# Alternating row and column stages in an inverse Haar and convolution round, with filter rows written in longer runs

## The chip, the cores and the metric

The kernel runs on one core of a Trainium2 chip. The metric is the device time of one execution in microseconds (us), the median of several. Five engines run side by side, each working through its own instructions in order: TensorE (PE in the profile; its weight loads are PEld), VectorE (DVE), ScalarE (ACT), GpSimd (POOL) and SyncE (SP). SyncE here only issues DMAs, and it issues nearly all of them. When the instruction at the head of an engine's queue waits for something, everything behind it on that engine waits too.

## The reference

The input x has 4 images of 64 channels of 256 x 256 float32 values. Four layers follow one another:

```python
x = conv(x, L0)      # y = filter * x  + bias * x
x = haar(x, L1)
x = conv(x, L2)
x = conv(x, L3)
```

In a `conv` layer each channel is convolved (causally, cut to 256 x 256) with an outer product of a column filter and a row filter of 256 values each. The filters come from a small network, three layers with a sine and a last product with `Xwo` or `Ywo`, times a decay:

```python
h = sin(freq * (z @ w1 + b1)); h = sin(freq * (h @ w2 + b2)); h = sin(freq * (h @ w3 + b3))
filter = (h @ wo) * exp(-t * abs(deltas))
```

The `haar` layer takes the two-dimensional Haar transform f1 of every channel; for each of two sets i it forms f4 = conv_w[i] mixed over channels of f1 * v[i], shrinks it to sign(f4) * max(|f4| - tau[i], 0), and adds both sets up. The inverse Haar transform of the sum, plus the layer's input, is the output. The Haar transform mixes rows and columns separately, so one direction can be a product with a matrix on TensorE and the other a chain of additions.

## The kernel before

**Units of work.** A round is two channels of two images, a tile of 128 partitions x 8 x 256 values (1 MB). There are 64 rounds (2 groups of images x 32 pairs of channels). A convolution of a round is two stages on TensorE, rows and columns. Each stage is a product with a Toeplitz matrix that is read from DRAM as overlapping slices of the filter (`load_toeplitz`, L146, tile `toep`, four buffers). Each stage is four pieces of 32 matmuls (`toeplitz`, L284); two pieces fill one PSUM group of two banks. After the second, the group is emptied: a row stage by ScalarE copies (L435, L830), a column stage by VectorE, which adds bias times the old value (`residual`, L455, L849). A Haar product is two pieces of eight matmuls (`haar`, L297).

**Phases.** Phase A runs rows and columns of layer 0, the forward additions on GpSimd (L336, L338), the forward product, and a store of the coefficients (`coef`). Phase B mixes channels and shrinks, step by step, for one group of images; it reads `coef` and writes `mixed`. Phase C runs the inverse additions on GpSimd (`inverse_free`, L377; `ci` is the result), the inverse product (P, `c0ps`), layer 2 (`c1r`, `c1c`) and layer 3 (`c2r`, `c2c`), and stores `out`. B for group 0 is interleaved with the second half of A, B for group 1 with the first 29 rounds of C; the rest of C runs alone. For group 1 most of the second set is stored unshrunk by B (`unshrunk`, L669) and is shrunk in the part of C that is alone (`shrink`, L754): a multiply (L772, VectorE), Sign and Abs (L774, L776, ScalarE), a subtraction and a threshold (L778, L781, VectorE), twice per round; GpSimd adds it to `g` (L797).

**Order.** Each phase is a list of small functions, pieces, and the order is written by hand: `beside` (L917) spreads one list evenly between the pieces of another. Nothing reorders instructions afterwards. Each piece first calls `flush` (L390), which emits the emptying of PSUM groups that earlier pieces left with `later`.

**An inverse round before.** In `piece` (L859) of phase C the order is: four row pieces of layer 2 of round t (R1), half of P of round t+1, four row pieces of layer 3 of round t-1 (R2), the other half of P, four column pieces of layer 2 of round t (C1), four column pieces of layer 3 of round t-1 (C2). The loads and stores stand at fixed pieces: `g` of round t+3 at the fifth, both Toeplitz tiles and the unshrunk tile at the sixth, `out` of round t-2 at the eighth. The shrinkage is at the first six pieces and again at the next six; scaling of `g` (`scales`, L350, seven ScalarE operations) is in the last seven pieces.

**PSUM.** Beside B, phase C's groups come from a ring of two; alone, from a ring of three (L955). A group can be written again once its earlier content has been emptied.

**Filters.** Each filter row is written to DRAM `REPEATS` = 20 times, so that a Toeplitz tile can be read as one strided pattern. `spread` (L245) writes one of three items for one of two halves at a time, in runs of 320 values (1280 bytes). The first two rounds' filters have their own path (`repeated`, L214). `last` (L222) is the final product of the filter network.

Of the kernel before, what the change touches and what calls it, by code (L numbers as in the profile page):

```python
# [70 lines left out]
ROUNDS = C // CI  # L71
STEPS = C
# [5 lines left out]
SHRINK = 6  # L78
# [17 lines left out]
def conv_haar_kernel(  # L96
    ctx: ExitStack, tc: tile.TileContext, x, zT, w1, wbd, cols, decay, wo_first, decay_first, bias, forward, inverse, wrow, pack, v, v_rows, out
# [73 lines left out]
    wbd_sb = [constant("wbd0", wbd[:, 0], [P, 3, P])]  # L171
    wo_first_sb = constant("wo_first", wo_first, [P, FIRST, COPIES])
    decay_first_sb = constant("decay_first", decay_first, [COPIES, FIRST, N])
    decay_sb = constant("decay", decay, [P, N])

    def network(ls):
# [45 lines left out]
        def last():  # L222
            ps = mps.tile([P, n, N], F32, tag="ps", name=f"mlp_out{ls[0]}")
            for e, l in enumerate(ls):
                nc.tensor.matmul(ps[:, e, :], wbd_sb[l][:, 2, :], st["h"][:, e, :], start=True, stop=True)
            padded = part("padded", PERIOD)
            nc.vector.memset(padded, 0.0)
            for e, l in enumerate(ls):
                nc.vector.tensor_tensor(padded[:, e, :N], ps[:, e, :], decay_sb, ALU.mult)
                filters[l] = padded[:, e, :]  # L230
# [7 lines left out]
        return pieces + [last]  # L238
# [6 lines left out]
    def spread(l, begin, end, parts):  # L245

        def put(r, k, channel, copies):
            src = filters[l][channel + CI * begin : channel + CI * (end - 1) + 1 : CI].unsqueeze(1)
            times = copies.stop - copies.start
            nc.sync.dma_start(filt[l][begin:end, r, copies, k], src.to_broadcast([end - begin, times, PERIOD]))  # L250

        n = REPEATS // parts
        pieces = []
        for c in range(parts):
            for r in range(2):
                for k in range(ITEMS):
                    channel = k if k < CI else C + r
                    pieces.append(lambda r=r, k=k, at=channel, c=c: put(r, k, at, slice(c * n, (c + 1) * n)))
        return pieces
# [13 lines left out]

    rest = spread(0, 8, 24, 2) + spread(0, 24, ROUNDS, 1)
    rest.append(lambda: wbd_sb.extend(constant(f"wbd{l}", wbd[:, l], [P, 3, P]) for l in (1, 2)))
    rest += network([1, 2])
    rest += spread(1, 0, ROUNDS, 5) + spread(2, 0, ROUNDS, 5)
# [133 lines left out]
    def phase_a():  # L411
# [63 lines left out]
        def piece(t, j):  # L475
            flush()
            if j == 0:
                if t == 0:
                    filters(0)
                    filters(1)  # L480
                    load(0)
                    load(1)
                    for put in spread(0, FIRST, 8, 1):
                        put()
                filters(t + 2)
# [237 lines left out]
    def phase_c():  # L723
# [30 lines left out]
        def shrink(t, k):  # L754
# [11 lines left out]
            if k == 0:  # L766
                s["shrunk"] = late["sb"].tile([P, 2 * M, N], F32, tag="shrunk", name=f"shrunk_{t}", bufs=2)
            for h in range(2):
                j = k - h * SHRINK
                if j == 0:  # L770
                    s["x"] = late["ps"].tile([P, NB, W], F32, tag="x", name=f"x_{t}_{h}")
                    nc.vector.tensor_tensor(s["x"], split("raw", h), rows(0, h), ALU.mult)  # L772
                elif j == 1:
                    nc.scalar.activation(split("shrunk", h), s["x"], AF.Sign)  # L774
                elif j == 2:
                    nc.scalar.activation(s["x"], s["x"], AF.Abs)  # L776
                elif j == 4:
                    nc.vector.tensor_tensor(s["x"], s["x"], rows(1, h), ALU.subtract)  # L778
                elif j == 5:
                    to = split("shrunk", h)  # L780
                    nc.vector.scalar_tensor_tensor(to, s["x"], 0.0, to, ALU.max, ALU.mult)  # L781

        def scaled(t, count):
            if 1 < t < total:
                run(st[t]["scales"], count)
# [72 lines left out]

        def piece(t, j):  # L859
# [5 lines left out]
            if j == 6 and t > 1:  # L865
                store(t - 2)
            if j == BLOCKS:
                filters(t + 1, 1)
                filters(t, 2)
            at = order.index(j)  # L870
            if t >= alone - AHEAD:
                if t == alone - AHEAD and at in (0, 2):
                    (load_raw(alone), load_rows()) if at == 0 else scale_rows()
                if j == BLOCKS:
                    load_raw(t + AHEAD + 1)
                shrink(t + AHEAD, at - 4 * (t == alone - AHEAD))
            if j == 2 * BLOCKS:

                load(t + 3)
            if j < BLOCKS:  # L880
                if t < total:
                    rows(t, 1, j)
            elif j < 2 * BLOCKS:
                if t > 0:
                    rows(t - 1, 2, j - BLOCKS)
            elif j < 2 * BLOCKS + 2:
                product(t + 1, j - 2 * BLOCKS)
            elif j < 3 * BLOCKS + 2:
                if t < total:
                    columns(t, 1, j - 2 * BLOCKS - 2)  # L890
            elif t > 0:
                columns(t - 1, 2, j - 3 * BLOCKS - 2)
            if at > 10 and t < total - 3 and "scales" in st[t + 3]:
                scaled(t + 3, 1 if t > 0 else 2)
# [181 lines left out]
```

## Time and profile before

| | |
|---|---|
| Median of 3 runs | 2650.2 us (2639.0 to 2656.2) |
| Profiled execution, own time | 2654.4 us |
| Its span, first to last instruction | 2652.6 us |
| TensorE matmuls busy | 2357.1 us (89%) |
| GpSimd busy | 2020.8 us (76%) |
| VectorE busy | 1785.2 us (67%) |
| ScalarE busy | 1325.2 us (50%) |
| Mean granted TensorE clock | 0.968 |
| DMA traffic | 684.6 MB, mean 258 GB/s |

In the trace the phases lie at about these places: start until 48 us (first round that runs without a break), A beside the writing of filters until 440, A beside B until 1087, the passage to C until 1224, C beside B until 1909, a passage until 1956, and C alone until the end. The phases have different limits, so a share over the whole span says little; windows of the trace, one for each phase, say more. In a line of groups, the first number is the start or busy time, the second the length, and "idle before" tells how long the engine stood still and what ended it. "issue" means that the profile shows nothing that the engine waited for.

### The profile page before, as it was taken

How to read it: one execution, taken by the hardware profiler on the slowest of the kernel's cores; microseconds unless marked ns; L12 is line 12 of the kernel's file. 1: busy time of each engine (PE TensorE's matmuls, PEld its weight loads, DVE VectorE, ACT ScalarE, POOL GpSimd, SP SyncE). 2: the span in 40 equal slices, each digit the busy share in tenths (PEclk: the TensorE clock that was granted, in tenths of full speed). 3: DMA queues.
4: the chain of work that ended last, by engine and by line, in shares of the span. 5: the costliest groups of instructions: out<-in, count | busy, mean ns of one | idle time of the engine just before them, and what ended most of it. 6: DMA issues, size and time to landing. Idle time of an engine off the chain costs nothing.

```text
span 2652.6 us, 117788 instructions
## 1 busy us (share of the span) xinstructions
PE 2357.1 (89%) x53276; PEld 1901.4 (72%) x53276; DVE 1785.2 (67%) x2040; ACT 1325.2 (50%) x2187; POOL 2020.8 (76%) x2426
## 2 busy tenths in 40 slices
PE   6999999678877778879999999999999999999999
PEld 5777777445554445657787777777888888888888
DVE  2564445799999999656565666665567767766663
ACT  1111112566666666236665566666555555555552
POOL 2788777889989889758666666666788898888881
PEclk9999999889999999889999999999999999999999
DMA  5767777699999889557888788988865566655552
GB/s 184 248 207 275 254 268 266 260 331 325 345 328 334 330 307 332 186 202 275 316 307 311 278 300 295 324 294 316 271 222 190 193 205 207 205 187 193 189 167 99
DMA packets 176006, 684.64 MB, mean 258 GB/s; under 512 B 22487, under 2 KB 35192, under 8 KB 151057
## 3 DMA queue, kind: packets, MB, share of 16 engines
q1 hardware_dynamic: 175505, 677.11, 72.5%
q8 instruction: 418, 6.85, 1.0%
q14 instruction: 83, 0.68, 0.1%
HBM read 427.40 MB, written 249.63 MB: 255 GB/s over the span
## 4 chain that ended last, share of the span: by engine, by line
PE 55%; DVE 15%; POOL 14%; issue 8%; ACT 5%; DMA 3%; SPq 1%; DVEq 0%; ACTq 0%; POOLq 0%
PE c1c L288 10%; PE c2c L288 10%; PE c2r L288 9%; PE c1r L288 8%; POOL fw L336 5%; PE f L596 4%; PE a2ps L288 4%; PE a1ps L288 4%; POOL f L338 4%; PE c0ps L300 3%; DVE a L632 3%; DVE x L455 2%; DVE x L615 2%; DVE m L637 2%; PE a3ps L300 2%
## 5 line engine op out<-in xcount | busy, mean ns | idle before, releaser
L377 POOL TENSOR_TENSOR i<-i,g 128x16 f32<-128x16 f32 x744 | 422.4, 588 | 27.8 <-ACT g L354 0.6
L596 PE MATMUL f<-ft,mix 64*64 64x512 f32 x2048 | 319.3, 641 | 104.7 <-DVE x L615 82.6
L288 PEld LDWEIGHTS a1ps<-toep,x 64*64 64x64 f32 x8192 | 306.1, 139 | 119.7 <-DVE f L468 42.1
L288 PEld LDWEIGHTS c1c<-toep,ch 64*64 64x64 f32 x8192 | 312.8, 134 | 86.5 <-ACT ch L830 35.2
L288 PEld LDWEIGHTS c2r<-toep,cy 64*64 64x64 f32 x8192 | 312.2, 134 | 77.0 <-issue 36.2
L288 PE MATMUL c1c<-toep,ch 64*64 64x192 f32 (+3 forms) x8192 | 337.8, 301 | 26.0 <-issue 13.4
L288 PE MATMUL a1ps<-toep,x 64*64 64x64 f32 (+3 forms) x8192 | 339.2, 308 | 24.1 <-DVE f L468 10.6
L288 PEld LDWEIGHTS a2ps<-toep,ay 64*64 64x64 f32 x8192 | 288.7, 135 | 92.4 <-issue 51.4
L288 PE MATMUL c2r<-toep,cy 64*64 64x192 f32 (+3 forms) x8192 | 330.4, 300 | 26.0 <-issue 22.7
L288 PE MATMUL a2ps<-toep,ay 64*64 64x192 f32 (+3 forms) x8192 | 325.7, 301 | 30.7 <-issue 22.1
L655 POOL TENSOR_TENSOR gt<-m,ft 128x512 f32<-128x512 f32 x128 | 163.4, 1277 | 235.8 <-DVE m L637 235.4
L455 DVE SCALAR_TENSOR_TENSOR x<-x,bias_sb,a2ps 128x512 f32<-128x512 f32 x256 | 179.6, 742 | 223.2 <-POOL f L338 114.9
L288 PE MATMUL c1r<-toep,z 64*64 64x192 f32 (+3 forms) x8192 | 316.5, 298 | 10.5 <-ACT g L354 8.0
L288 PEld LDWEIGHTS c1r<-toep,z 64*64 64x64 f32 x8192 | 297.3, 134 | 38.3 <-issue 15.6
L288 PE MATMUL c2c<-toep,ch 64*64 64x256 f32 (+3 forms) x8192 | 316.9, 297 | 7.9 <-issue 7.5
L377 POOL TENSOR_TENSOR ci<-i,g 128x1024 f32<-128x1024 f32 x124 | 319.8, 2600 | 4.5
L435 ACT COPY ay<-a1ps 128x512 f32<-128x512 f32 x256 | 137.1, 588 | 372.3 <-PE a1ps L288 371.9
L621 ACT ACTIVATE m<-x 128x1024 f32<-128x1024 f32 x194 | 206.1, 1062 | 229.6 <-DVE x L615 170.5
L288 PEld LDWEIGHTS c2c<-toep,ch 64*64 64x64 f32 x8192 | 297.6, 134 | 32.0 <-issue 18.3
L632 DVE TENSOR_TENSOR a<-a,v 128x1024 f32<-128x1024 f32 x192 | 235.5, 1226 | 54.6 <-ACT a L627 54.6
L849 DVE SCALAR_TENSOR_TENSOR cy<-z,bias_sb,c1c 128x512 f32<-128x512 f32 x256 | 177.5, 741 | 136.9 <-PE c1c L288 136.8
L627 ACT ACTIVATE a<-x 128x1024 f32<-128x1024 f32 x194 | 199.9, 1030 | 122.6 <-DVE m L637 122.6
(80 smaller groups left out, 3782.5 us busy)
## 6 DMA issues: line engine op xcount, KB each, us to landing
toep<-filt SPq DMA_DIRECT2D x384, 224.0 KB, 6.1
coef<-f SPq DMA_DIRECT2D x128, 512.0 KB, 6.7
ft<-coef SPq DMA_DIRECT2D x128, 512.0 KB, 7.9
v<-in_v SPq DMA_DIRECT2D x64, 1024.0 KB, 7.2
mixed<-gt SPq DMA_DIRECT2D x128, 512.0 KB, 6.9
g<-mixed SPq DMA_DIRECT2D x128, 512.0 KB, 7.6
x<-in_x SPq DMA_DIRECT2D x63, 1024.0 KB, 6.7
out<-o SPq DMA_DIRECT2D x63, 1024.0 KB, 8.8
```

Source lines behind the costliest of these rows:

```text
L288: nc.tensor.matmul(ps[r][half(c), j % 2, k * ROW :], data[half(r), c, k, bass.ts(j, ROW)], t(r, c)[:, : N - k * ROW], start=k == 0, stop=k ...
L300: nc.tensor.matmul(ps[r][half(c)].rearrange("p h k -> p (h k)"), matrix[half(r)], pairs(r, c).rearrange("p h k -> p (h k)"), start=True, s ...
L336: nc.gpsimd.tensor_tensor(diffs, even, odd, ALU.subtract)
L377: engine.tensor_tensor(to, s, d, op)
L435: later(lambda y=y, ps=ps: nc.scalar.copy(y, ps))
L455: nc.vector.scalar_tensor_tensor(to, old, bias_sb[:, c : c + 1], ps, ALU.mult, ALU.add)
L596: nc.tensor.matmul(un[u]["f4"][half(q), b, :], mixers[0][half(r), bass.ts(i, C)], st[s]["f"][half(r), b], start=True, stop=True, tile_posi ...
L621: nc.scalar.activation(un[u]["m"], un[u]["x"], AF.Sign)
L627: nc.scalar.activation(un[u]["a"], un[u]["x"], AF.Abs)
L632: nc.vector.tensor_tensor(un[u]["a"], un[u]["a"], both(u, "tau"), ALU.subtract)
L655: nc.gpsimd.tensor_tensor(g[:, 0], m[:, 0], st[s]["f"][:, 0], ALU.add)
L849: nc.vector.scalar_tensor_tensor(to, of, bias_sb[:, at : at + 1], ps, ALU.mult, ALU.add)
```

## The change

1. The order in an inverse round becomes R1 (four pieces), first half of P, C2 of round t-2 (four), R2 of round t-1 (four), second half of P, C1 of round t (four). Layer 3's columns thus run one round later than before, and there is one more round of pieces at the end.
2. The shrinkage's ten operations stand at pieces 1, 2, 3, 5, 6 and 10, 11, 12, 14, 15. The scaling of `g` is at pieces 8 (three operations), 9 (two), 15 and 16 (one each).
3. The DMAs of a round are issued at other pieces: `g` at 1, layer 2's Toeplitz tile at 2, the unshrunk tile at 5, `out` at 10, layer 3's Toeplitz tile at 13.
4. `spread` writes all three items of both halves in one DMA, in runs of 960 values (3840 bytes). To have these side by side in one partition, `last` makes three products per layer with 64 output rows in place of one with 128, in pieces of their own, from a separate constant `wo`.

```diff
-SHRINK = 6
+SHRINK = (1, 2, 3, 5, 6, 10, 11, 12, 14, 15)
...
-        def last():
-            ps = mps.tile([P, n, N], F32, tag="ps", name=f"mlp_out{ls[0]}")
-            for e, l in enumerate(ls):
-                nc.tensor.matmul(ps[:, e, :], wbd_sb[l][:, 2, :], st["h"][:, e, :], start=True, stop=True)
-            padded = part("padded", PERIOD)
-            nc.vector.memset(padded, 0.0)
-            for e, l in enumerate(ls):
-                nc.vector.tensor_tensor(padded[:, e, :N], ps[:, e, :], decay_sb, ALU.mult)
-                filters[l] = padded[:, e, :]
+        def last(e, k):
+
+            l = ls[e]
+            if k == 0:
+                filters[l] = mp.tile([HALVES, ITEMS, PERIOD], F32, tag=f"padded{l}", name=f"padded{l}")
+                nc.vector.memset(filters[l], 0.0)
+            ps = mps.tile([HALVES, N], F32, tag="ps", name=f"mlp_out{l}_{k}")
+            nc.tensor.matmul(ps, wo_sb[:, l, k], st["h"][:, e, :], start=True, stop=True)
+            nc.vector.tensor_tensor(filters[l][:, k, :N], ps, decay_sb[:, k], ALU.mult)
...
-        def put(r, k, channel, copies):
-            src = filters[l][channel + CI * begin : channel + CI * (end - 1) + 1 : CI].unsqueeze(1)
-            times = copies.stop - copies.start
-            nc.sync.dma_start(filt[l][begin:end, r, copies, k], src.to_broadcast([end - begin, times, PERIOD]))
+        def put(copies):
+            at = slice(2 * begin, 2 * end)
+            src = filters[l][at].rearrange("p k e -> p (k e)").unsqueeze(1)
+            to = filt[l].rearrange("t h c k e -> (t h) c (k e)")[at, copies]
+            nc.sync.dma_start(to, src.to_broadcast([2 * (end - begin), copies.stop - copies.start, SPAN]))
...
-    rest = spread(0, 8, 24, 2) + spread(0, 24, ROUNDS, 1)
+    rest = [p for q in (8, 16, 24) for p in spread(0, q, q + 8, 2)]
...
-    rest += spread(1, 0, ROUNDS, 5) + spread(2, 0, ROUNDS, 5)
+    rest += spread(1, 0, ROUNDS, 10) + spread(2, 0, ROUNDS, 10)
...
-                    for put in spread(0, FIRST, 8, 1):
+                    for put in spread(0, FIRST, 8, 2):
...
+        R1, C2, R2, C1 = 0, BLOCKS + 1, 2 * BLOCKS + 1, 3 * BLOCKS + 2
+
         def piece(t, j):
             flush()
             if j == 0:
                 if t == 0:
                     load(2)
                 sums(t + 2)
-            if j == 6 and t > 1:
+            if j == (BLOCKS if t == 0 else 1):
+                load(t + 3)
+            if j == 2:
+                filters(t + 1, 1)
+            if j == C2 + BLOCKS + 1 and t > 1:
                 store(t - 2)
-            if j == BLOCKS:
-                filters(t + 1, 1)
+            if j == R2 + BLOCKS:
                 filters(t, 2)
...
-                if j == BLOCKS:
+                if j == BLOCKS + 1:
                     load_raw(t + AHEAD + 1)
-                shrink(t + AHEAD, at - 4 * (t == alone - AHEAD))
-            if j == 2 * BLOCKS:
-
-                load(t + 3)
-            if j < BLOCKS:
+                shrink(t + AHEAD, j - 2 * first)
+            if R1 <= j < R1 + BLOCKS:
                 if t < total:
-                    rows(t, 1, j)
-            elif j < 2 * BLOCKS:
-                if t > 0:
-                    rows(t - 1, 2, j - BLOCKS)
-            elif j < 2 * BLOCKS + 2:
-                product(t + 1, j - 2 * BLOCKS)
-            elif j < 3 * BLOCKS + 2:
+                    rows(t, 1, j - R1)
+            elif C2 <= j < C2 + BLOCKS:
+                if 1 < t:
+                    columns(t - 2, 2, j - C2)
+            elif R2 <= j < R2 + BLOCKS:
+                if 0 < t <= total:
+                    rows(t - 1, 2, j - R2)
+            elif j >= C1:
                 if t < total:
-                    columns(t, 1, j - 2 * BLOCKS - 2)
-            elif t > 0:
-                columns(t - 1, 2, j - 3 * BLOCKS - 2)
-            if at > 10 and t < total - 3 and "scales" in st[t + 3]:
-                scaled(t + 3, 1 if t > 0 else 2)
-            if t == 0 and at > 0:
-                scaled(2, 1)
+                    columns(t, 1, j - C1)
+            else:
+                product(t + 1, int(j > BLOCKS))
+            if t == 0:
+                scaled(3, 2 * (2 * BLOCKS <= j < C1))
+                scaled(2, int(j > 0))
+            else:
+                scaled(t + 3, {8: 3, 9: 2, 15: 1, 16: 1}.get(j, 0))
...
-        first, second, last = range(BLOCKS), range(BLOCKS, 2 * BLOCKS), range(2 * BLOCKS + 2, C_PIECES)
-        order = [*first, 2 * BLOCKS, *second, 2 * BLOCKS + 1, *last]
...
-        pieces = [lambda t=t, j=j: piece(t, j) for t in range(total + 1) for j in order]
+        pieces = [lambda t=t, j=j: piece(t, j) for t in range(total + 2) for j in range(C_PIECES)]
```

## The prediction

> **What bounds the kernel now.** I read the table of stages first (TensorE, its weight loads, VectorE, ScalarE, GpSimd: busy time; clock; DMA share; GB/s):
>
> ```profile
> 48.00:440.00 392.00, 361.06 (x8888) 300.08 (x8892) 188.79 (x283) 72.58 (x135) 307.44 (x514) 1.00 0.71 247
> 440.00:1087.00 647.00, 514.91 (x8474) 318.38 (x8470) 595.80 (x622) 394.67 (x492) 576.36 (x644) 0.92 0.87 317
> 1224.00:1909.00 685.00, 645.03 (x14664) 533.20 (x14659) 425.64 (x450) 417.81 (x734) 453.52 (x542) 1.00 0.85 304
> 1956.00:2601.00 645.00, 615.73 (x16378) 568.05 (x16371) 444.43 (x490) 344.13 (x640) 552.04 (x557) 0.99 0.58 192
> ```
>
> Row 2, the forward rounds beside the first shrinkage, is VectorE's (92% busy), and the change does not touch it. Rows 3 and 4, the inverse rounds beside the second shrinkage and alone, are TensorE's (94% and 95%). So the question is what stops TensorE there. The chain of waits, TensorE only, in row 4's window:
>
> ```profile
> PE c2r L288 <- issue: 10.4, 7, 3.2
> PE c1c L288 <- issue: 9.4, 13, 2.2
> PE c1c L288 <- ACT ch L830: 9.0, 7, 1.9
> ```
>
> Two thirds of the idle time has no releaser at all. One such stop, from the timeline (start, length; idle before), with what SyncE issued ahead of it, and the page's line on the instruction queue:
>
> ```profile
> 2060.66 1.26 SPq L742 DMA_DIRECT2D raw<-unshrunk  x2
> 2062.02 0.54 SPq L856 DMA_DIRECT2D out<-o  x1
> 2062.66 1.77 SPq L736 DMA_DIRECT2D g<-mixed  x2
> 2067.04 2.35 DVE L772 TENSOR_TENSOR x<-raw,rows 128x1024 f32<-128x1024 f32 x1
> ...
> 2069.12 0.28 PE L288 MATMUL c2r<-toep,cy 64*64 64x64 f32 x3 [1.13 <-issue]
> ```
>
> ```profile
> q8 instruction: 418, 6.85, 1.0%
> ```
>
> 6.85 MB in 418 packets is 16 KB, 256 instructions of TensorE, each. In the DMA records the packet before this stop started at 2066.41 and took 1.20; TensorE went on 1.5 later. All stops without a releaser end 1.2 to 1.6 us after such a packet lands. Counting instructions, a packet can start when 256n+190 have run; in the window alone 128 packets start 1.9 us after that on average, and about 3 us late is what TensorE bears. Lateness follows the bytes SyncE has issued that have not moved: under 0.5 MB, 0 of 74 packets are over 3 us late; 0.5 to 1.5 MB, 7 of 20; over 1.5 MB, 30 of 34. The excess over 3 us sums to 37 us.
>
> First matmul to first matmul, a round alone takes 5.23 (R1 and half the Haar product), 5.78 (R2 and the other half), 5.41 (C1), 4.39 (C2) = 20.8; the shortest of each make 19.2. Beside the shrinkage it is 26.4, of which 19.2 and 4.6 units of 0.87 us explain 23.2. So 1.6 and 3.2 us a round are to be had, no more: 53 and 90 us.
>
> [...] L772 takes 1.23 alone and 2.35 here, beside GpSimd's 2.85 us ci operations.
>
> **The change, part by part.**
>
> *Start.* TensorE idles 7.1 us up to 48.0 for x(2). SyncE issues six writes of filter rows (6.76 us, to 31.0); they move at 6.4 busy engines of 16, since six SBUF rows feed each, and hold toep(2), the next writes and x(2) (issued 40.69). Two writes of twelve rows take some 2 us to issue and should land at 32 to 33 instead of 38.1; x(2) comes 6 us earlier. Column work ends at 40.9, so the gain is at most 7.1: I take −6 (0 to −7).
>
> *Writing filter rows.* 84 issues become 28, 11,520 packets of 1280 bytes (59 ns) become 3,840 of 3840 bytes; the nearest row is 3584 bytes, 155 median to 196 mean. 42 us of sixteen engines become 37 to 47: nothing, behind a DMA share of 0.71. But the twenty writes of 491 KB now lie in rounds 22 to 33, one in 5.5 pieces: 3.3 MB a round for 2.9, and instructions wait on that. The last network layer becomes six matmul pieces for VectorE's one or two, each with VectorE waiting in order on TensorE ahead of the residuals (one such wait is 4.8 now); VectorE is 48% busy here, GpSimd 78%. In the start they end near 22.8, under the wait for toep until 24.2. Together +3 (−3 to +7).
>
> *First inverse round.* R1(1) waits at 1158.6 for toep, 7.96 us. The change loads it ahead of g(3), which cures that; but scaling of g(3) (landing near 1165, 2.5 us of ScalarE) now stands ahead of the second product's copies on ScalarE, so R1(1) starts at about 1169.5 for 1166.6: +3 (−3 to +6).
>
> *Alternation, ScalarE and VectorE.* Today ScalarE empties six PSUM groups in a row (R1, R1, P, R2, R2, P), with Sign and Abs between, and VectorE four. A Sign that waits for L772 holds up the copies behind it, and C1 waits for R2's: 7 stops, 9.0 us. After, the order is R1, P, C2, R2, P, C1; each engine empties two or three groups and then has four pieces for the rest. The shrinkage's multiply stands in row stages, where VectorE has no residual; its subtraction and threshold (1.2 each) stand ahead of residuals, with 2 us of room by the ring of three groups. −0.25 us a round alone, −0.3 beside the shrinkage, where ten group boundaries lose about 1.8.
>
> *Alternation, SyncE.* Today one run of issues follows C1 and C2: toep 0.9, raw 1.0, out 1.0, g 1.0 MB. After, SyncE stops twice a round: toep for conv 1 (0.45) waits for C1's end, raw (1.0) follows; out waits for C2's residual, now mid-round (about 11 us), then toep (0.45) and g (1.0). Two runs of 1.45 and 2.45 MB. A run drains at about 250 GB/s (last g: 2.4 MB, 9.5 to 10.4 us), so time above 1.5 MB falls from 5 to some 1.3 us a round, and time at 0.5 to 1.5 grows. Excess lateness goes from 1.2 to about 0.7: −0.5 a round. Beside the shrinkage 28 stops (25 us idle[...]) are 1.4 a round; with g and toep half a round from out I take −0.6. Nothing is late for that: g lands at 25 us for scaling at 27 in the next round alone, and beside the shrinkage keeps its seven pieces; out's wait holds the shrinkage's loads behind it on SyncE by up to 2 us, which have a step to spare.
>
> Alone 33 × −0.75 = −25 (−8 to −45); beside 28 × −0.9 = −25 (−5 to −45). An extra round at the end holds C2(63) only; the order R2(63), C2(63) was the last one before.
>
> Sum: −6 +3 +3 −25 −25 = −50. The profiled execution took 2654.4 (span 2652.6 and 1.8 around it), 4.2 above the median: 2604 there, **2600** as median.
>
> **Rivals.**
> - *The runs of issues only move* (25%). 3.9 MB a round at 250 GB/s is 81% of 19.2 us however it is split; the second run may meet the next first one. For it: lateness over 3 us begins near 1 MB. Against it: the 5 us above 1.5 MB. Then only ScalarE's part stays: −8 alone, −8 beside, −6 +6: 2634, about 1% and so hardly to be told from no change.
> - *GpSimd becomes the bound, slower* (9%). Its chain in a round alone (adds L797, inverse, ci) runs 18.7 us from 2052.9 to 2071.6, with ci at 2.85 for 2.38 uncontended. If VectorE's operations, now spread over the whole round, hold it up more, it decides from 20.8 us a round on; at 22 the stage gives +40 over 33 rounds, with the rest 2682. Against it: it now waits 68 us in the window for ScalarE's last scale, which comes two pieces earlier, and VectorE's work is the same.
> - *Nearly all stops go* (6%): 19.3 alone, 24.5 beside: −103, 2547.
>
> **Numbers.** Forecast 60%, own range 2575 to 2625. Faster by over 1% (under 2624; about what three runs from 2639 to 2656 can tell): 55 of the forecast, 6, and 3 of the first rival: 0.64. Slower by over 1%: 0.09. Range 2570 to 2650: the bounds of the two −25 taken together reach it, and leave out the last two rivals.
>
> **What would show it.** First matmul of round 2 near 42 instead of 48. In the window alone: rounds of 20.0 (20.8), "c1c <- ACT" near 0, "issue" waits halved, g and out issued half a round from raw. Beside: rounds of 25.5. Wrong if "issue" stops stand unchanged behind the new second run, if ScalarE waits on g's landing at its scales ahead of R2's copies, or if TensorE waits on ci.

## The result: no change that can be told, and three stages that moved a lot

The changed kernel took 2659.6 us (median of 20 runs, 2644.7 to 2663.7) beside 2653.6 for the kernel before: a ratio of 1.0015, 95% interval 0.9999 to 1.003. The forecast was 2600 with a range of 2570 to 2650; it was wrong. Line numbers of the changed kernel are some three lower than before (the helper of the toeplitz products is L285 for L288, ScalarE's row copies L826 for L830).

The table of stages of the changed kernel (TensorE, its weight loads, VectorE, ScalarE, GpSimd: busy time; clock; DMA share; GB/s) has the windows that the prediction read:

```profile
48.00:440.00 392.00, 356.30 (x8653) 292.09 (x8657) 187.74 (x280) 70.36 (x131) 299.27 (x500) 0.98 0.72 244
440.00:1087.00 647.00, 510.82 (x8586) 316.53 (x8582) 593.21 (x619) 391.46 (x489) 574.92 (x645) 0.93 0.87 318
1224.00:1909.00 685.00, 635.70 (x14440) 530.23 (x14436) 422.56 (x445) 413.92 (x729) 452.13 (x536) 0.99 0.84 299
1956.00:2601.00 645.00, 634.25 (x17033) 593.48 (x17029) 488.83 (x510) 361.15 (x669) 574.73 (x576) 1.00 0.62 203
```

(A window is fixed while the phases shift by some us, so the table shows loads, and the next one lengths.) In the last row TensorE does more matmuls in the same 645 us than before (17,033 for 16,378): the stage alone got faster. In the first and third row it does fewer. First matmuls, read from the two traces, give each stretch a length:

| stretch | before, us | after, us | difference | forecast |
|---|---|---|---|---|
| start to round 2 | 48.0 | 51.9 | +3.9 | −6 |
| round 2 to round 34 (beside the filter work) | 386.1 | 393.3 | +7.2 | +3 |
| round 34 to round 62 of the forward part, at 1087.4 / 1098.9 (beside the first shrinkage) | 653.3 | 653.7 | +0.4 | 0 |
| from there to R1 of round 3 (passage) | 136.5 | 140.6 | +4.1 | +3 |
| R1 of round 3 to R1 of round 29, beside the shrinkage | 685.6 | 693.5 | +7.9 | −25 (28 rounds) |
| R1 of round 29 to 31 | 46.7 | 49.5 | +2.8 | |
| R1 of round 31 to 63, alone | 664.2 | 637.2 | −27.0 | −25 (33 rounds) |
| R1 of round 63 to the end | 32.2 | 37.7 | +5.5 | |
| whole span | 2652.6 | 2657.4 | +4.8 | −50 |

The last C2 stage, some 4.4 us, moved from the passage to the end, which is in the +4.1 and the +5.5.

**Alone**, TensorE's waits in the changed kernel (total, times, longest) are these; the prediction showed 10.4, 9.4 and 9.0 for the kernel before:

```profile
PE c1c L285 <- issue: 3.8, 4, 1.4
PE c1r L285 <- issue: 2.3, 4, 1.0
PE c2c L285 <- issue: 2.2, 5, 0.7
PE c1c L285 <- ACT ch L826: 1.2, 5, 0.3
```

**Beside the shrinkage** the waits without a releaser changed place, not size. In the window 1224 to 1909 the kernel before has

```profile
PE c2r L288 <- issue: 11.5, 10, 2.4
PE c2c L288 <- issue: 7.5, 9, 1.2
```

and the changed kernel

```profile
PE c1r L285 <- issue: 15.8, 13, 2.3
PE c2c L285 <- issue: 6.9, 8, 2.4
PE c1c L285 <- ACT ch L826: 4.6, 5, 1.5
```

Lateness of instruction packets says the same. It is counted as in the prediction: how long after TensorE's count of instructions allows it a packet starts, summed for what is over 3 us. From R1 of round 31 to that of round 63 it fell from 37 to 8 us, and 34 packets with more than 1.5 MB outstanding became at most 2. From round 3 to round 29 it stayed at 89 us, and of some 116 packets 40 met more than 1.5 MB before and 41 after.

**The start** is on the chain of the work that ended last (start, length, what). Before:

```profile
29.80 8.33 DMA filt<-padded
...
40.69 7.20 DMA x<-in_x
48.03 6.31 PE a1ps L288 x112
```

After:

```profile
24.79 14.30 DMA filt<-padded
...
40.99 10.83 DMA x<-in_x
51.91 5.98 PE a1ps L285 x112
```

The second of the two new writes is issued at 24.8 us, 5 us before the last of the six old ones. It lands 1 us later than that, at 39.1, and the load of x(2), issued behind the next write, takes 10.8 us for 7.2.

### The profile page after: what moved, and what is told of

It reads as the page before. It is cut to its first block, busy times and chain, and to the rows that moved or that the text cites. A ratio compares the mean times of both kernels' runs of the same rounds, so it can differ in the third digit from the quotient of the medians.

```text
span 2657.4 us, 117725 instructions
## 1 busy us (share of the span) xinstructions
PE 2354.2 (89%) x53288; PEld 1907.8 (72%) x53288; DVE 1825.4 (69%) x2047; ACT 1325.1 (50%) x2187; POOL 2021.5 (76%) x2426
## 4 chain that ended last, share of the span: by engine, by line
PE 54%; DVE 15%; POOL 13%; issue 6%; DMA 5%; ACT 5%; SPq 1%; DVEq 0%; ACTq 0%; POOLq 0%
PE c2c L285 9%; PE c1c L285 9%; PE c2r L285 9%; PE c1r L285 9%; POOL fw L333 5%; PE f L593 5%; POOL f L335 4%; PE a1ps L285 4%; PE a2ps L285 4%; PE c0ps L297 3%; DVE a L629 2%; DVE x L452 2%; DVE x L612 2%; DVE m L634 2%; POOL gt L649 2%
## 5 line engine op out<-in xcount | busy, mean ns | idle before, releaser
L374 POOL TENSOR_TENSOR i<-i,g 128x16 f32<-128x16 f32 x744 | 400.5, 559 | 27.9 <-ACT g L351 0.8
L593 PE MATMUL f<-ft,mix 64*64 64x512 f32 x2048 | 319.9, 632 | 107.9 <-DVE x L612 83.5
L285 PEld LDWEIGHTS a1ps<-toep,x 64*64 64x64 f32 x8192 | 309.4, 141 | 127.9 <-issue 55.3
L285 PE MATMUL a1ps<-toep,x 64*64 64x192 f32 (+3 forms) x8192 | 345.3, 313 | 29.7 <-DMA x<-in_x 9.4
L285 PEld LDWEIGHTS c2c<-toep,ch 64*64 64x64 f32 x8192 | 311.8, 134 | 66.5 <-issue 22.6
L285 PEld LDWEIGHTS c1c<-toep,ch 64*64 64x64 f32 x8192 | 313.5, 134 | 60.8 <-ACT ch L826 27.9
L285 PE MATMUL c1r<-toep,z 64*64 64x256 f32 (+3 forms) x8192 | 325.7, 299 | 31.7 <-issue 21.5
L285 PEld LDWEIGHTS a2ps<-toep,ay 64*64 64x64 f32 x8192 | 283.9, 134 | 89.9 <-issue 47.1
L285 PE MATMUL a2ps<-toep,ay 64*64 64x192 f32 (+3 forms) x8192 | 321.9, 300 | 27.2 <-issue 17.9
L285 PEld LDWEIGHTS c1r<-toep,z 64*64 64x64 f32 x8192 | 304.1, 134 | 56.7 <-issue 31.4
L285 PE MATMUL c2c<-toep,ch 64*64 64x128 f32 (+3 forms) x8192 | 329.8, 299 | 15.0 <-issue 9.2
L285 PE MATMUL c1c<-toep,ch 64*64 64x256 f32 (+3 forms) x8192 | 328.1, 299 | 14.4 <-ACT ch L826 9.9
L285 PEld LDWEIGHTS c2r<-toep,cy 64*64 64x64 f32 x8192 | 299.7, 134 | 26.8 <-issue 11.0
L285 PE MATMUL c2r<-toep,cy 64*64 64x256 f32 (+3 forms) x8192 | 315.3, 298 | 4.1 <-issue 2.3
L333 POOL TENSOR_TENSOR fw<-x 128x1024 f32<-128x1024 f32 x64 | 121.3, 1896 | 195.2 <-DVE x L452 190.4
L826 ACT COPY ch<-c2r 128x512 f32<-128x512 f32 x256 | 137.7, 592 | 254.9 <-PE c2r L285 254.6
```

Of the source, the lines that this page charges most:

```text
L285: nc.tensor.matmul(ps[r][half(c), j % 2, k * ROW :], data[half(r), c, k, bass.ts(j, ROW)], t(r, c)[:, : N - k * ROW], start=k == 0, stop=k ...
L333: nc.gpsimd.tensor_tensor(diffs, even, odd, ALU.subtract)
L374: engine.tensor_tensor(to, s, d, op)
L593: nc.tensor.matmul(un[u]["f4"][half(q), b, :], mixers[0][half(r), bass.ts(i, C)], st[s]["f"][half(r), b], start=True, stop=True, tile_posi ...
L826: later(lambda y=y, ps=ps: nc.scalar.copy(y, ps))
```

## Experiments

Ratios are to the kernel before, with the 95% interval; us by round are from the one profiled execution of each kernel.

### The two parts apart

The first kernel is the one before with the hunks of the change that write filter rows; the second is the changed kernel with those hunks undone.

```diff
-    rest = spread(0, 8, 24, 2) + spread(0, 24, ROUNDS, 1)
+    rest = [p for q in (8, 16, 24) for p in spread(0, q, q + 8, 2)]
...
-    rest += spread(1, 0, ROUNDS, 5) + spread(2, 0, ROUNDS, 5)
+    rest += spread(1, 0, ROUNDS, 10) + spread(2, 0, ROUNDS, 10)
```

> The inverse rounds of before with only the filter rows written the new way (runs of 3840 bytes from neighbouring rows). Theory S, that the writing alone costs what round 34 is late in the trace of after: first matmul of round 2 near 52 us (48.0 before), of round 34 near 445 (434.1 before), everything after that as before, so about +11 on the whole. Theory of the prediction, that the writing is worth -3: round 2 near 42, round 34 near 431. Rival, that the two parts of the change disturb each other and neither alone costs anything at the start: round 34 near 434, whole +0.

> The alternating inverse rounds of after with the filter rows written as before (runs of 1280 bytes). Theory S: round 2 near 48, round 34 near 434, and from there on the stages of after: passage +8, beside the second shrinkage 26.6 us a round as in after, alone 19.9; the whole about 11 below after, 5 or so below before. Rival, that the slow rounds beside the shrinkage come from the other writing too: they go to 25.5 us a round and the whole to about -35 against before.

The new rows alone: 1.0049 (1.0029 to 1.0068), slower by 13 us; round 2 at 52.7, round 34 at 450.5. The new rounds alone: 0.9960 (0.9943 to 0.9976), faster by 11 us (some 5 were expected); round 2 at 46.7, beside the shrinkage 26.65 a round, alone 19.88. So the writing alone loses what the inverse rounds gain; the sum of the two, +2, is close to the +4 of both together, so they hardly disturb each other, and the slower rounds beside the shrinkage are the alternation's own. One miss: round 34 came at 441.9 in the second kernel, not 434; since its round 5 is at 83.5, that lies in rounds 5 to 34, which took from 344 to 358 us over all the traces.

### What makes the writes slow

In the kernel before, `put` takes every second row (step CI = 2), so the six rows of a write lie two partitions apart; in the changed kernel its rows are neighbours. Three kernels, each the changed one with the writing altered. First the run length: the same neighbouring rows, each write in three.

```diff
-            src = filters[l][at].rearrange("p k e -> p (k e)").unsqueeze(1)
-            to = filt[l].rearrange("t h c k e -> (t h) c (k e)")[at, copies]
-            nc.sync.dma_start(to, src.to_broadcast([2 * (end - begin), copies.stop - copies.start, SPAN]))
+            to = filt[l].rearrange("t h c k e -> (t h) c k e")[at, copies]
+            for k in range(ITEMS):
+                src = filters[l][at, k].unsqueeze(1)
+                nc.sync.dma_start(to[:, :, k], src.to_broadcast([2 * (end - begin), copies.stop - copies.start, PERIOD]))
```

> The kernel after, with the same neighbouring rows, but each write split in three of 1280-byte runs. Theory P: still slow, since the same 12 rows feed it: the last write of rounds 2 to 8 lands at 37 or later, round 2 begins at 51 or later, round 34 near 445. Rival L (run length): packets of 1280 bytes go at 55 to 60 ns as before, round 2 near 48, round 34 near 434, the whole 11 below after.

Ratio 0.9983 (0.9965 to 1.0002); round 2 at 54.9, round 34 at 445.2, the last of the first writes landed at 39.7. The DMA totals from 33 to 36 us are the same for both lengths. The changed kernel:

```profile
DMA packets 62, 0.23 MB, mean 77 GB/s; under 512 B 2, under 2 KB 2, under 8 KB 62
```

Its rows in short runs:

```profile
DMA packets 186, 0.23 MB, mean 78 GB/s; under 512 B 15, under 2 KB 185, under 8 KB 185
```

Three times the packets, the same bytes. A packet of 3840 bytes takes 573 ns there (median, 32 to 36 us) and one of 1280 bytes 181, while the kernel before moves 1280 bytes in 55. It is not the length of the run. Nor are neighbours slow at once: of the first 80 of the changed kernel's 240 packets most took 149 ns, and they moved at 112 to 240 GB/s; the 573 ns, and 69 to 86 GB/s, set in at about the hundredth and last nearly to the end.

Then where the rows lie. In the first kernel the rows are cut and placed anew (groups of eight, four partitions apart, the groups over all 128 partitions):

```diff
+def place(i):
+    return 4 * (i % 8) + 64 * (i // 8 % 2) + i // 16
...
-        def put(copies):
-            at = slice(2 * begin, 2 * end)
-            src = filters[l][at].rearrange("p k e -> p (k e)").unsqueeze(1)
+        def put(i, n):
+            p = place(i)
+            src = filters[l][p : p + 4 * n - 3 : 4].rearrange("p k e -> p (k e)").unsqueeze(1)
```

> The kernel after, runs of 3840 bytes as they are, but the 64 filter rows of a layer lie four partitions apart in groups of eight, and eight groups of them over all 128 partitions, so that one write of layer 0 reads 8 rows (or 4) far apart instead of 12 or 16 neighbours. Theory P, that a write is slow [...]: 12 neighbours move at some 78 GB/s, so 4 and 8 spread rows together should move at 150 GB/s or more; the two first writes land within 8 us of their issue (14.3 in after), round 2 begins near 45 (51.9), round 34 near 432 (445), the whole 10 to 14 below after. Rival L, that the long run itself is slow: 14 us, 52, 445, and no change of the whole.

Ratio 0.9924 (0.9901 to 0.9947), 20 us below the kernel before and 24 below the changed one (10 to 14 were expected; 14 of them are there at round 34, the rest is not traced); round 2 at 46.9, round 34 at 431.4. Packets took 149 ns. But the two first writes landed at 37.4, 12.9 after their issue and not within 8; only about five DMA engines worked on them at a time (33.9% of 16 busy from 32 to 36 us). Still the first toeplitz load came early (issued at 34.8 for 39.2), as it waits there for the small write of four rows alone. Cut and place were mixed, so the next kernel changes the place only: every second partition.

```diff
-            src = filters[l][at].rearrange("p k e -> p (k e)").unsqueeze(1)
+            src = filters[l][4 * begin : 4 * end - 1 : 2].rearrange("p k e -> p (k e)").unsqueeze(1)
```

> The kernel after with one thing changed: the 64 filter rows of a layer lie on every second partition instead of on neighbouring ones, so that a write has the same rows, copies, runs of 3840 bytes and issue as in after, but its 12 rows span 24 partitions instead of 12 (16 rows span 32). It takes out of the kernel with rows over all partitions what was mixed there: other cuts of rows, and a write of 4 rows that the first load of toeplitz rows waits for alone. Theory P [...] between 32 and 36 us 140 to 165 GB/s instead of 78, packets near 290 ns instead of 573, round 2 at 47 to 49 (51.9), round 34 at 432 to 437 (445), the whole 9 to 12 below after. Rival (rows in a write, not where they lie): 78 GB/s, 573 ns, 52, 445.

From 31 to 32 us the DMA totals of the changed kernel, and then of this one, are

```profile
DMA packets 23, 0.08 MB, mean 84 GB/s; under 512 B 1, under 2 KB 1, under 8 KB 23
DMA packets 74, 0.28 MB, mean 284 GB/s; under 512 B 0, under 2 KB 0, under 8 KB 74
```

The last of the same 240 packets, with the same 12 rows for each write, ended at 33.6 instead of 38.7. At full rate they move at 296 GB/s (77 with neighbours once these have slowed), with 149 to 191 ns a packet in the median. Only from 31.5 us on do some take up to 300. Round 2 began at 45.0, 6.9 earlier than in the changed kernel. So it is where the rows lie that decided here, and more strongly than the 140 to 165 GB/s that were the author's estimate. The whole moved less than expected: 0.9990 (0.9973 to 1.0007), about 6 us below the changed kernel's ratio, with round 34 at 438.7.

Sixteen rows differed in the same way. The next write of the changed kernel has 16 neighbours, and from 43 to 46 us

```profile
DMA packets 83, 0.32 MB, mean 106 GB/s; under 512 B 0, under 2 KB 0, under 8 KB 83
```

were moved, at some 575 ns a packet; two later writes of 16 rows on every second partition moved 1.2 MB from 44.1 to 48.5 us, 279 GB/s, at 149 ns a packet. A write longer than these 4.4 us was not tried, and what it is about neighbours that slows them was not shown.

### Why nothing was gained beside the shrinkage

Both kernels, before and after, with less data in the inverse rounds. They leave out the stores of out (but for three rounds) and of unshrunk, so the result is not the reference's:

```diff
-            to, g = step_of(unshrunk, s, st[s]["raw"])
-            nc.sync.dma_start(to, g)
...
-                for rows, to in all_rows(unshrunk, t % ROUNDS, r):
+                for rows, to in all_rows(mixed[1], t % ROUNDS, r):
...
-            if t < total - 1:
+            if t < 2:
                 nc.sync.dma_start(out[t // ROUNDS, t % ROUNDS], st[t]["y"])
```

> The kernel before without two transfers of the inverse rounds: the stores of out (1.0 MB a round; only the first two rounds and the last are stored) and the stores of unshrunk (some 1.2 MB a round beside the second shrinkage); the loads of raw take as many bytes from mixed instead, so that the values, not the work, of the last rounds differ. Theory V, that late instruction packets follow the volume of data: beside the shrinkage, lateness over 3 us falls from 90 us to under 45 and a round from 26.4 to about 25.7; alone, from 37 to under 15 us and a round from 20.8 to about 20.2, with the 9 us of TensorE waiting for ScalarE's copies ahead of C1 still there. Rival (the stops come from the order of the engines): 26.4 and 20.8 as before.

> The kernel after without the same two transfers (out in all but the first two and the last round, unshrunk altogether, raw read from mixed). Theory V: beside the shrinkage the packets come on time once 2.2 of some 8 MB a round are gone: lateness over 3 us from 87 to under 40 us, waits without a releaser from 28 us to under 15, a round from 26.7 to 25.9 or less; alone little is left to gain, 19.9 to 19.8. Rival (in after the stops beside the shrinkage come from VectorE's shrinkage standing among the residuals, not from traffic): a round stays at 26.5 or more.

| | before | before, less data | after | after, less data |
|---|---|---|---|---|
| beside, us a round | 26.37 | 25.65 | 26.67 | 25.43 |
| beside, lateness over 3 us, us in all | 89 | 36 | 89 | 15 |
| alone, us a round | 20.76 | 20.09 | 19.91 | 19.59 |
| alone, lateness over 3 us, us in all | 37 | 6 | 8 | 2 |

The windows beside the shrinkage and alone (columns as above; DMA share next to last), first before with less data, then after with less data:

```profile
1228.00:1895.00 667.00, 638.35 (x14688) 538.71 (x14684) 424.85 (x450) 417.98 (x734) 454.90 (x543) 1.00 0.68 225
1941.00:2584.00 643.00, 633.11 (x16904) 590.18 (x16900) 446.59 (x500) 349.49 (x650) 552.65 (x557) 1.00 0.45 144
```

```profile
1245.00:1906.00 661.00, 634.57 (x14672) 532.44 (x14668) 426.13 (x450) 417.56 (x734) 456.63 (x544) 0.99 0.68 226
1957.00:2583.00 626.00, 622.71 (x16882) 587.75 (x16878) 473.38 (x500) 350.16 (x650) 556.94 (x558) 1.00 0.46 148
```

At a DMA share of 0.68 instead of 0.84 most packets beside the shrinkage come on time: those that meet more than 1.5 MB outstanding fall from 40 to 13 in the kernel before, and from 41 to 7 in the changed one. At full volume SyncE has more than 1.5 MB outstanding in a third of all cases with either order, and lateness is the same. With less data the changed kernel has less lateness than the kernel before (15 us for 36) and is 0.2 us a round ahead. That is what the alternation does alone, but traces of one order with full data differ by 0.2 to 0.3 a round too, so this gain is not proven. Leaving the stores out also shortens the runs of issues and takes SyncE's wait for out away; the runs don't part this from the volume itself. The wholes were 0.9869 (0.9831 to 0.9906) and 0.9900 (0.9864 to 0.9935). One expectation missed: alone, before with less data, the wait for ScalarE's copies ahead of C1 fell to 3.1 us and did not stay at 9.

### Order against runs of issues, alone

To tell what splitting the issues is worth, SyncE's issues were put together again in the changed kernel, compute order untouched. The first try moved out behind the loads of g and the toeplitz rows of conv 2 beside those of conv 1, from round 4 on:

```diff
             if j == 2:
                 filters(t + 1, 1)
+                if t > 3:
+                    filters(t - 1, 2)
+            if j == 1 and t > 3:
+                store(t - 3)
...
-            if j == R2 + BLOCKS:
+            if j == R2 + BLOCKS and t < 3:
                 filters(t, 2)
```

> The kernel after, compute order untouched, but from round 4 on SyncE's issues stand together again: the store of out waits for the next round, where it follows the loads of g at the round's beginning, and the toeplitz rows of conv 2 are loaded there too, beside those of conv 1, instead of behind C2 in the middle of the round. Theory L, that part of the gain alone is from splitting the run: lateness over 3 us alone back from 8 to 20 or more, waits without a releaser from 8 us to 15 or more, a round alone 20.2 to 20.4 (19.9). Rival O, that the gain alone is all from the order of the stages (ScalarE's and VectorE's emptying in smaller groups): 19.9 to 20.0. Beside the shrinkage, where splitting did not lower lateness, both expect 26.5 to 26.8.

Ratio 1.0128 (1.0102 to 1.0154); alone 20.17, lateness 13.7; beside the shrinkage 27.37, against the 26.5 to 26.8 that both theories gave. It did not make one run: out still went alone in mid-round, ahead of a wait, and the toeplitz rows then came so late beside the shrinkage that TensorE waited for them. The second try starts at round 32 and puts the rows of conv 1 first:

```diff
+            once = t >= alone
...
             if j == 2:
                 filters(t + 1, 1)
+                if once:
+                    load(t + 3)
+                    filters(t - 1, 2)
+                    if t > alone:
+                        store(t - 3)
...
-            if j == R2 + BLOCKS:
+            if j == R2 + BLOCKS and t < alone - 1:
                 filters(t, 2)
```

> The kernel after, compute order untouched; only from round 32 on SyncE's issues stand behind one wait: the toeplitz rows of conv 1, which wait for the end of C1, come first, and g, the toeplitz rows of conv 2 and out follow at once, so that a round issues some 3.9 MB in one run as before (1.45 and 2.45 MB in after). Theory L, that splitting the runs is a part of the gain alone: lateness over 3 us alone from 8 to 25 or more, waits without a releaser from 7 us to 15 or more, a round 20.2 to 20.4 (19.9 in after, 20.8 before). Rival O, that the order of the stages is all of it: 19.9 to 20.0. In both the stages up to round 31 are those of after.

SyncE's issues in one round of the changed kernel (start, length, what):

```profile
2102.88 1.79 SPq L155 DMA_DIRECT2D toep<-filt  x2
2104.76 1.27 SPq L739 DMA_DIRECT2D raw<-unshrunk  x2
2114.58 0.34 SPq L852 DMA_DIRECT2D out<-o  x1
2115.01 1.96 SPq L155 DMA_DIRECT2D toep<-filt  x2
2117.08 1.29 SPq L733 DMA_DIRECT2D g<-mixed  x2
```

and with the second try:

```profile
2104.14 1.18 SPq L155 DMA_DIRECT2D toep<-filt  x2
2105.41 0.53 SPq L852 DMA_DIRECT2D out<-o  x1
2106.04 1.95 SPq L739 DMA_DIRECT2D raw<-unshrunk  x2
2113.73 1.19 SPq L155 DMA_DIRECT2D toep<-filt  x2
2115.02 1.27 SPq L733 DMA_DIRECT2D g<-mixed  x2
```

There are still two runs, because the toeplitz rows of conv 2 wait for C2; out has joined the other one, so that they are 2.45 and 1.45 MB where they were 1.45 and 2.45. That is enough: lateness 22 us (8), waits without a releaser 19.5 us between round 31 and 63 (6.6 in after), 20.28 us a round (19.91), whole 1.0058 (1.0041 to 1.0074). Lateness missed the 25 that was expected of it; the round met its 20.2 to 20.4. Moving 1.0 MB from one run to the other costs 0.37 us a round; in eight other traces with the alternation a round alone took 19.71 to 20.04. So the order of the stages is not all of the gain, and it matters where out is issued. What one run of 3.9 MB would cost with this order was not measured, and why the same two sizes the other way round are worse stays open.

### The passage

```diff
             if t == 0:
-                scaled(3, 2 * (2 * BLOCKS <= j < C1))
                 scaled(2, int(j > 0))
+            elif t == 1:
+                scaled(3, 2 * (0 < j <= BLOCKS))
+                scaled(4, 2 * (j >= C1))
             else:
```

> The kernel after, with the scaling of g(3) moved from round 0 behind the copies of the second Haar product (into the row pieces of round 1), and that of g(4) into the column pieces of round 1. Theory: the stop of 9.3 us in the middle of R1(1) is ScalarE standing at a scale for g(3) with the product's copies queued behind; it goes, R2(0) begins 6 to 9 us earlier after R1(1) (24 us in after), and the whole is 5 to 9 below after. Rival: the stop turns into a wait for the toeplitz rows or for g(4), and the whole gains less than 2.

ScalarE in the changed kernel (start, busy, what; idle before it and its releaser) stands at a scale for 7.55 us with copies of the second Haar product behind it:

```profile
1173.13 1.18 ACT L814 COPY z<-c0ps 128x512 f32<-128x512 f32 x2 [6.60 <-PE c0ps L297]
1181.86 2.50 ACT L351 ACTIVATE g<-g 128x16 f32<-128x16 f32 x7 [7.55 <-DMA g<-mixed]
1184.27 1.04 ACT L814 COPY z<-c0ps 128x512 f32<-128x512 f32 x2
```

TensorE waits for those copies in the middle of R1(1):

```profile
PE c1r L285 <- ACT z L814: 9.3, 1, 9.3
```

With the scales later, TensorE's two longest waits from 1147 to 1217 are

```profile
PE f L593 <- DVE ft L572: 7.8, 2, 5.0
PE c0ps L297 <- ACT ch L826: 4.5, 1, 4.5
```

The stop of 9.3 us is gone. In its place TensorE stands at the next product behind ScalarE, and then at the first product of the shrinkage, whose input waits for loads that were issued behind the last round of the forward part. R2(0) begins 22.2 us after R1(1) instead of 23.8, and the whole is at 1.0010 (0.9995 to 1.0025). The rival was right in the main: most of the wait turned into others.

### Put together

The last two kernels have the rows over all partitions, the old order of stages up to round 28 and the alternation from round 29 on. They differ in round 0: the first loads toeplitz rows ahead of g(3), the second keeps the issue order of before.

```diff
+        switch = ROUNDS - AHEAD
+        together = [*range(C2), *range(R2, C_PIECES), *range(C2, R2)]
...
+            if t < switch:
+                return early(t, j)
...
-                if 1 < t:
+                if t > switch:
                     columns(t - 2, 2, j - C2)
```

Here early is the round of before: R1, half the product, R2, the other half, C1, C2.

> Both parts arranged by what the runs say: filter rows in runs of 3840 bytes spread over all partitions; the inverse rounds in the old order (C1 and C2 one after the other) up to round 28, beside the shrinkage, and alternating from round 29 on; in round 0 the toeplitz rows are loaded ahead of g(3). Theory: round 34 near 431, passage 3 to 8 shorter than before, beside 26.2 to 26.4 a round, alone 19.9: about -33 against before, 12 below the alternating rounds with spread rows. Rival, that the alternation beside the shrinkage costs nothing by itself: as spread rows with alternation, -21.

> The kernel with spread filter rows, old order up to round 28 and alternation from 29 on, with round 0's issues as in before (g(3) ahead of the toeplitz rows). If loading the toeplitz rows first in round 0 is what made the passage 5.7 us longer there (first R1 of round 0 to that of round 3: 88.6 for 82.9), it returns to 83 to 84 and the whole goes to about -29 against before (-24 to -26 in the kernel with the other issue order); else it stays at 88 and -24.

They took 0.9907 (0.9882 to 0.9932) and 0.9893 (0.9865 to 0.9922), about 24 and 28 us below the kernel before: faster than both kernels of this case. The first missed the 33 us that were expected of it: the old order beside the shrinkage was to bring 12 us over the alternating rounds with spread rows. It brought about 4, which is within the two intervals. Beside the shrinkage a round took 26.33 and 26.27, alone 19.90 and 19.71. R1(0) to R1(3) took 88.6 with the toeplitz rows first and 85.1 with g(3) first. It was 82.9 before, but 85.9 in the kernel with the old rounds and the new rows, so it is only a hint that loading the rows earlier made the passage longer. The second kernel's table of stages, beside and alone:

```profile
1224.00:1909.00 685.00, 649.43 (x14750) 540.76 (x14745) 429.09 (x453) 420.42 (x738) 459.03 (x546) 1.00 0.86 304
1956.00:2601.00 645.00, 640.82 (x17328) 600.16 (x17323) 477.95 (x505) 354.10 (x658) 554.32 (x557) 1.00 0.60 198
```

Alone TensorE is busy 640.8 of 645 us.

## Why the prediction was wrong, step by step

- *Start, −6.* Wrong. The step that failed is "they move at 6.4 busy engines of 16, since six SBUF rows feed each": the count of rows was taken for the whole limit. Twelve rows did put 11.2 engines to work (mean from 30 to 37 us), but after about a hundred packets each at a quarter of its speed (573 ns a packet for 149), because the rows are neighbours. With the same rows on every second partition the landing is 33.6, close to the forecast of 32 to 33. Neighbours made it 39.1, and round 2 came 3.9 later instead of 6 earlier. Even with the early landing it came only 3.0 earlier than before (45.0), so the gain was put too high as well.
- *Writing filter rows, +3.* Right where the rows are many, wrong for layer 0. Rounds 5 to 34, with the 64-row writes of layers 1 and 2, took 347.9 us for 350.4 (344 to 358 over all traces), so no loss to them shows. But the later writes of layer 0, 16 neighbours each, lie in rounds 2 to 5, which took 45.4 us for 35.7: +9.7 that the sum did not have. With rows two apart these rounds took 40.4, and with neighbours in short runs 40.5, so where the rows lie is not shown to be all of it. The 3840-byte packet was priced from a 3584-byte row of other transfers (155 to 196 ns); it took 573 at the start, and 149 in the median of the whole run.
- *Passage, +3.* The mechanism was right and its size too small. ScalarE stands at g(3)'s scale ahead of the product's copies, as forecast. The estimate kept g(3)'s landing of before, near 1165. R1(0) began 12.9 us later for the reasons above, and g(3) was issued 16.3 us later, behind the toeplitz rows that the change puts ahead of it. The stop was 9.3 us for 8.0, and another 3.9 us went at the first product of the shrinkage (1.8 before). With the C2 stage that left the passage the loss is 8.5. The experiment shows why no single wait is the price: with this one away R1(0) to R1(3) was 2.2 us shorter, and over the seven traces with the change's rounds and full data that stretch took 81.7 to 85.6 anyway.
- *Beside the shrinkage, −25.* Wrong: +7.9. The step that failed is "with g and toep half a round from out I take −0.6": it carried the gain of the stage alone, where the DMA share is 0.6, into a stage of 0.85, where 299 GB/s in 26.7 us is 8 MB a round. Lateness stayed at 89 us, as many packets as before met more than 1.5 MB outstanding, and only with 2.2 MB a round less did it fall. The forecast's 1.4 us a round for stops is more than the 25 us of idle time show (under 1.0 over 26 rounds); the rest was the author's estimate. The order's −0.3 is not visible at full volume. Over the seven traces with alternation and full data, out's issue as in the change, rounds took 26.42 to 26.72 (mean 26.59), over the four with the old order 26.13 to 26.37 (26.28). What makes alternation 0.3 slower there is only partly seen: 0.1 is one stop of 5 us for ci in the first of these rounds (2 us with the old order); 0.1 to 0.2 is C1 waiting for ScalarE's copies, 4.2 to 5.9 us in all against 0 to 1.1 with the old order, a wait that the change was to lessen; and waits without a releaser are 0.92 to 1.09 us a round (mean 1.03), with the old order 0.68 to 0.99 (mean 0.85). These sum to somewhat more than 0.3, so other waits became shorter. Lateness is 82 to 89 us in the seven and 64 to 89 in the four; why packets about as late should cost more is open.
- *Alone, −25.* Right: −27.0. The split was not. Order was put at −0.25 and lateness at −0.5; with less data the two orders still differ by 0.50 (20.09 to 19.59; lateness, 6 and 2 us, is about 0.1 of it), and issuing out elsewhere gives back 0.37. So order is worth some 0.4 to 0.5 and the issues about as much. The shares are not sharp, since two traces of the old rounds differ by 0.26 (20.76, and 20.50 with the new rows). The order's worth was underrated: first matmul to first matmul C1 takes 4.7 for 5.4, and R2 with its half product 5.2 for 5.8 (R1 and C2 take 0.1 and 0.2 more), while the named wait for ScalarE was only 9 us in all. That wait was a weak measure too: with the same old rounds and the new rows it was 1.8.
- *Nothing for the extra round at the end.* As forecast for the sum: +5.5 there, −4.4 in the passage.

Against the forecast of −50 the span came out 54.8 higher: 33 from the rounds beside the shrinkage, 14 from the start and the filter work, 10 from the passage and the other short stretches, 2 less from the stage alone. The first rival, that the runs of issues only move, was the nearest beside the shrinkage, and the runs with less data fit its reason, the volume. It was wrong alone. GpSimd did not become the bound; alone it is busy 575 of 645 us, and TensorE's waits there name it nowhere. (That rival's 2682 does not follow from its own terms: +40 alone and the other four as forecast make +15, or 2665.)

## What to carry to other kernels

Read a queueing gain against the DMA share of the stage that it is to work in: the new order of stages and issues brought lateness down at a share of 0.6 (37 to 8 us) and not at 0.85 (89 and 89), where it fell only with fewer bytes (to 15 at a share of 0.68). When a transfer reads a few SBUF rows many times, look at which partitions these rows are on before counting packets or bytes; here the time of a packet in the nearest row of the profile (155 to 196 ns) did not hold for neighbours (573), and 149 to 191 ns was measured for rows two apart. And where one wait is cured in a start-up stretch, list who else stands behind the same loads: of 9 us that left one place, at most 2 stayed gained in the passage.

## What the runs showed of the hardware that was not expected

Twelve neighbouring SBUF rows, read by DMA, moved at 77 GB/s once some hundred packets had gone faster (the first 80 at 112 to 240); the same twelve on every second partition moved at 296 GB/s, with nothing else changed. Run length made no difference to the bytes moved (77 and 78 GB/s with runs of 3840 and 1280 bytes). Rows four partitions apart, in groups of eight, had fast packets too (149 ns) but kept only about five engines busy and moved at 142 GB/s from 32 to 36 us; why these were fewer was not tested. Beside the next slow write the load of x(2) took 10.8 us for 7.2.
